# Broadcast rows of a selective scan: sixteen copies in DRAM instead of four, and one DMA instead of two for the group that mixes two directions

## The chip, the cores and the metric

The kernel runs on one core of a Trainium2 chip. The metric is the device time of the program in microseconds (us), the median of three runs. The profile is of one execution. Engines are named as in the profile: PE is TensorE, DVE is VectorE, ACT is ScalarE, POOL is GpSimd, and SP is SyncE, which here does nothing but issue DMAs; "SPq" is its queue of issues.

## The reference, cut to what matters

The program takes two images of 96 channels and 128 x 128 pixels. It normalizes over channels, adds the result of a four-direction selective state-space layer (a Mamba block for each direction, fused by one linear layer), and then runs two quantized feed-forward layers with a 3 x 3 convolution between them. The part that matters here is the scan of one direction over its L = 16384 positions, with 192 inner channels d and 16 states s:

```
xc  = silu(causal_conv4(x @ in_w.T))           # (L, 192)
dt  = softplus(xc @ Wdt + dt_b)                # (L, 192), through a rank of 6
B,C = xc @ xproj_w.T                           # (L, 16) each: the same for all channels d
h[d,s] = exp(dt[d] * A[d,s]) * h[d,s] + dt[d] * xc[d] * B[s]     # step after step
y[d]   = sum_s h[d,s] * C[s]
```

B and C depend on the position and the state, but not on the channel. With channels on partitions, a row B[s, :] has to stand on every partition.

## The kernel before

**Tiles.** For each image there are two passes (`pi`), each over a pair of directions: one along rows of the image, one along columns. Two times 192 channels make three groups of 128 partitions (`NG = 3`): group 0 is 128 channels of the first direction, group 2 is 128 channels of the second, and group 1, the middle one, has 64 channels of the first on partitions 0 to 63 and 64 of the second on 64 to 127. The positions are cut into 32 tiles of T = 512. So a pass has 32 steps, an image 64, the program 128.

**Steps and units.** A step is worked off in 24 units: three groups times eight pairs of states. One unit is, for 128 partitions and two states:

- POOL, `b_part` (L324): dt * xc * B, in place on the B rows, 128 x 1024;
- ACT, `decay` (L330): exp(dt * A), two instructions, into PSUM;
- DVE, `scan` (L334): two recurrences of 512 positions, one for each state;
- DVE (L409): h * C, 128 x 1024, in place on the C rows;
- ACT (L410): the last column of h, kept for the next step;
- PE, `sums` (L341): two matmuls by the identity, which add up over states in PSUM (`y`); a new `y` begins with L416, at the first unit of each group, and the old one is then multiplied by the gate on DVE (L349).

**Where the rows come from.** Once a step, the part of the prologue named `rows` computes all B and C rows of the next step: 64 of them (2 kinds, B or C; 2 directions; 16 states), on partitions 32 to 95 of the tile `rows`. `rows_out` copies them from PSUM and writes them to a DRAM tile, `bcd` (L261), four times over (`COPIES = 4`), with four DMAs of all 64 partitions. `row_tile` (L320) then fetches a quad, which is four states of B or of C and so enough for two units: 8 KB on each of 128 partitions, 1 MB. For groups 0 and 2 this is one DMA, whose source is read with a step of 0 so that the partitions take the four copies in turn. For group 1 it is two DMAs of 64 partitions, since the two halves read rows of different directions.

**Order.** Every engine's order is written out by hand (`manual_schedule`); SP issues DMAs in that order and waits at each for its buffer. The main loop runs over units k, and the fetches and the prologue of the next step are placed by unit:

```
if k % 2 == 0:
    fetch(k + 2 * B_AHEAD, 0, B_AHEAD, bs)      # B of units k+6, k+7; four buffers
feed(k + AHEAD)                                 # b_part of unit k+2
...                                             # scan, multiply of unit k-1, scan
if k % 2 == 0:
    fetch(k + 2 * C_AHEAD, 1, C_AHEAD, cs)      # C of units k+4, k+5; three buffers
```

`rows_out` of the next step stands at the end of unit 12 of a step. Unit 18 is the first that issues a fetch for the next step. Around the write SP's order is: B for unit 18, C for unit 16, the four writes of `bcd`, B for unit 20, C for unit 18, B for unit 22, C for unit 20, B for the next step's unit 0.

Of the kernel before, what the change touches and what calls it, by code (L numbers as in the profile page):

```python
# [10 lines left out]
F32 = mybir.dt.float32  # L11
# [12 lines left out]
T = 512  # L24
NT = L // T
R = T // W
S = 16
# [2 lines left out]
HID = 384  # L30
PAIRS = ((0, 2), (1, 3))
NG = 3
COPIES = 4
B_AHEAD = 3
C_AHEAD = 2
AHEAD = 2
# [1 line left out]
BCO = 32  # L38
NBC = 4 * S
# [3 lines left out]
def tile_metaformer(ctx: ExitStack, tc: tile.TileContext, a: dict, out: bass.AP):  # L43
    nc = tc.nc
# [138 lines left out]
    def mamba(acc, xnr, xnc):  # L183

        with ExitStack() as st:
# [3 lines left out]
            rows_d = pool("rows_d", 3, space=DRAM)  # L189
# [20 lines left out]
            def prologue(pi, i, d):  # L210
# [3 lines left out]
                src = []  # L214
# [40 lines left out]
                def rows_out():  # L255

                    d["rows"] = one.tile([BCO + NBC, T], F32, name="rows")
                    nc.scalar.copy(d["rows"], d["ps"][0 : BCO + NBC, :])
                    d["bcd"] = rows_d.tile([COPIES, 2, NBC // 2, T], F32, name="bcd")
                    for n in range(COPIES):  # L260
                        nc.sync.dma_start(d["bcd"][n].rearrange("k r t -> (k r) t"), d["rows"][BCO:, :])  # L261

# [35 lines left out]

                at = [(0, 0, load), (8, 1, partial(silu, "xc")), (14, 1, partial(silu, "sz"))]
                at += [(12, 0, rows), (12, 1, rows_out)]
                for g, k in enumerate((4, 5, 6)):
                    at += [(k, 0, partial(conv, g)), (k, 1, partial(conv_out, g))]
# [7 lines left out]
            def row_tile(d, g, s, k, ahead):  # L312

                t = gen.tile([128, 4, T], F32, name=f"row{k}", bufs=ahead + 1)
                for half in range(2) if g == 1 else (slice(None),):
                    rows = slice(half * 64, half * 64 + 64) if g == 1 else half
                    at = s + S * (half if g == 1 else g // 2)
                    n = (64 if g == 1 else 128) // COPIES
                    src = d["bcd"][None, :, k, at : at + 4, :].broadcast_to((n, COPIES, 4, T))
                    nc.sync.dma_start(t[rows], src)  # L320
                return t

            def b_part(d, g, b):
# [62 lines left out]
            def fetch(k, n, ahead, m):  # L386
                if k < total:
                    t = row_tile(state[k // nu], *units[k % nu], n, ahead)
                    m[k], m[k + 1] = t[:, 0:2, :], t[:, 2:4, :]
# [46 lines left out]
            for k in range(total + 6):  # L436
                n, u = divmod(k, nu)
# [185 lines left out]
```

## Time and profile before

| what | value |
|---|---|
| time, median of 3 runs | 13002.54 us (12999.16 to 13004.72) |
| profiled execution | 13002.5 us, TensorE clock 0.963 |
| busy | PE 83%, DVE 89%, ACT 66%, POOL 71% |
| scan, L334 | 5952 in 7339.4 us (mean 1274 ns), and a smaller form for the first step of a pass |
| multiply by C, L409 | 3072 in 3705.9 us (mean 1206 ns) |
| B part on POOL, L324 | 3072 in 7175.7 us (mean 2358 ns) |
| rows, 1 MB DMAs | 2048, 7.5 us from issue to landing (median) |
| rows, 512 KB DMAs | 2048, 8.0 us |
| `bcd` writes, 128 KB | 512, 9.8 us |
| DMA | 3400 MB in all, mean 262 GB/s, packets' time 83.1% of 16 engines' span |
| HBM | read 3288.94 MB, written 104.86 MB |

The page gives busy time for each engine, the costliest groups of instructions by line, and for each group how long its engine stood idle before it and what ended that. The wait tables sum such idle times by who waited for whom. "DMA share" in a window is the time that packets took on the core's 16 DMA engines, as a share of the window; a packet that takes longer because it shares a path counts longer. A landing time counts from the issue on SP and so includes the time behind earlier DMAs in the rings.

### The profile page before, as it was taken

What the parts mean: (1) busy time and instruction counts of PE and PEld (TensorE: products, weight loads), DVE (VectorE), ACT (ScalarE), POOL (GpSimd) and SP (SyncE); (2) the same over time, 40 slices, a digit from 0 to 9 for tenths busy, and PEclk for the clock granted to TensorE, in tenths of its full rate; (3) what the DMA queues carried; (4) which work ended last, traced back from release to release, by engine and by line L of the source; (5) the groups of instructions that cost most, each with busy time, mean ns of one, the idle gap of its engine ahead of it and who ended that gap; (6) DMA issues with size and microseconds to landing.
All of it is one profiled execution on the core that took longest, in us unless ns stands there. A gap on an engine that the chain in (4) does not pass through costs nothing. (4 is left out here: it accounts for less than half of the span.)

```text
span 13002.5 us, 97992 instructions
## 1 busy us (share of the span) xinstructions
PE 10850.3 (83%) x24208; PEld 3987.1 (31%) x24208; DVE 11569.1 (89%) x10865; ACT 8560.0 (66%) x14738; POOL 9215.4 (71%) x4772
## 2 busy tenths in 40 slices
PE   6888888888888888888978888888888888888889
PEld 2323233333333333333323333332333333333233
DVE  5999999999999999995459999999999999999954
ACT  6666666666666666665566666666666666666655
POOL 4877778777787787772147778777787777877721
PEclk8999999999999999999989999999999999999999
DMA  7999999999999999992079999999999999999920
GB/s 226 287 294 282 298 288 285 295 283 298 288 285 295 283 295 289 285 295 68 13 226 285 298 283 292 290 285 298 285 291 291 284 298 286 290 294 281 296 61 13
DMA packets 545331, 3400.40 MB, mean 262 GB/s; under 512 B 81612, under 2 KB 82732, under 8 KB 146840
## 3 DMA queue, kind: packets, MB, share of 16 engines
q1 hardware_dynamic: 544760, 3394.12, 83.1%
q8 instruction: 195, 3.19, 0.1%
q14 instruction: 376, 3.08, 0.1%
HBM read 3288.94 MB, written 104.86 MB: 261 GB/s over the span
## 5 line engine op out<-in xcount | busy, mean ns | idle before, releaser
L324 POOL TENSOR_TENSOR row<-dtu,row 128x1024 f32<-128x1024 f32 x3072 | 7175.7, 2358 | 1739.3 <-DMA row<-bcd 1419.2
L334 DVE TENSOR_TENSOR_SCAN da<-da,hst,row 128x512 f32<-128x512 f32 x5952 | 7339.4, 1274 | 351.2 <-ACT da L330 194.6
L341 PE MATMUL y<-row,ident 128*128 128x512 f32 x12288 | 6120.1, 626 | 1113.3 <-DVE row L409 1098.9
L330 ACT ACTIVATE da<-dt,amat 128x512 f32<-128x512 f32 x6144 | 4249.4, 692 | 207.5 <-ACT hst L410 0.4
L341 PEld LDWEIGHTS y<-row,ident 128*128 128x128 f32 x12288 | 2288.9, 197 | 4779.4 <-DVE row L409 2292.3
L409 DVE TENSOR_TENSOR row<-da,row 128x1024 f32<-128x1024 f32 x3072 | 3705.9, 1206 | 19.6 <-DMA row<-bcd 18.8
L410 ACT COPY hst<-da 128x2 f32<-128x2 f32 x3072 | 484.0, 158 | 2235.5 <-DVE row L409 2233.3
L416 PE MATMUL y<-xc,dmat 128*128 128x512 f32 x768 | 526.1, 773 | 779.1 <-DVE sz L349 779.1
L287 POOL TENSOR_TENSOR q<-e,q 128x512 f32<-128x512 f32 x384 | 488.0, 1271 | 821.8 <-ACT hst L410 709.1
L233 ACT ACTIVATE xc<-misc,convb 128x512 f32<-128x512 f32 x384 | 264.2, 688 | 1117.5 <-PE misc L207 1117.5
L207 PE MATMUL misc<-xa,inx 96*128 96x512 f32 (+1 forms) x2048 | 932.4, 597 | 59.0 <-DMA xa<-xnr 57.2
L207 PE MATMUL misc<-xb,inx 96*64 96x512 f32 (+1 forms) x2048 | 928.1, 595 | 1.6 <-ACT xc L233 1.6
L531 POOL TENSOR_TENSOR acc<-acc,y 96x512 f32<-96x512 f32 x128 | 147.6, 1153 | 987.0 <-DVE y L530 987.0
L541 PE MATMUL pc<-pad,kw 96*96 96x512 f32 x1152 | 566.7, 593 | 0.0
L207 PEld LDWEIGHTS misc<-xa,inx 96*128 96x128 f32 (+1 forms) x2048 | 323.6, 163 | 625.5 <-issue 493.4
L293 POOL TENSOR_TENSOR dt<-dt,ln 128x512 f32<-128x512 f32 x384 | 486.9, 1268 | 30.1
L297 POOL TENSOR_TENSOR dtu<-dt,xc 128x512 f32<-128x512 f32 x384 | 488.5, 1272 | 0.5
L290 POOL TENSOR_TENSOR ln<-ln,q 128x512 f32<-128x512 f32 x384 | 488.1, 1271 | 0.5
L359 PE MATMUL misc<-sz,gmat 128*96 128x512 f32 x1024 | 483.6, 594 | 0.0
L416 PEld LDWEIGHTS y<-xc,dmat 128*128 128x128 f32 x768 | 129.0, 211 | 1102.1 <-DVE sz L349 1099.1
L268 PE MATMUL misc<-rows,dtw 12*128 12x512 f32 x768 | 439.7, 652 | 18.5 <-ACT dt L275 17.2
L132 DVE TENSOR_TENSOR xq<-xm,rs 96x512 fp8e5<-96x512 f32 x128 | 87.9, 687 | 387.8 <-ACT rs L128 387.8
(75 smaller groups left out, 8403.8 us busy)
## 6 DMA issues: line engine op xcount, KB each, us to landing
row<-bcd SPq DMA_DIRECT2D x2048, 1024.0 KB, 7.5
row<-bcd SPq DMA_DIRECT2D x2048, 512.0 KB, 8.0
bcd<-rows SPq DMA_DIRECT2D x512, 128.0 KB, 9.8
xa<-xnr SPq DMA_DIRECT2D x124, 193.1 KB, 5.8
xb<-xnc SPq DMA_DIRECT2D x124, 193.1 KB, 5.5
acc<-in_x_dram SPq DMA_DIRECT2D x16, 768.0 KB, 17.8
xnr<-xn SPq DMA_DIRECT2D x16, 768.0 KB, 4.3
xnc<-stg SPq DMA_DIRECT2D x16, 768.0 KB, 5.6
```

Of the source, the lines that this page charges most:

```text
L207: nc.tensor.matmul(ps[rows, :], w(PAIRS[pi][d], k, lo, hi), src[d][:, k : k + T], **se)
L287: nc.gpsimd.tensor_tensor(d["q"], d["e"], d["q"], ALU.subtract)
L290: nc.gpsimd.tensor_tensor(d["ln"], d["ln"], d["q"], ALU.add)
L293: nc.gpsimd.tensor_tensor(d["dt"][g], d["dt"][g], d["ln"], ALU.add)
L297: nc.gpsimd.tensor_tensor(dtu, d["dt"][g], d["xc"][:, g, :], ALU.mult)
L324: nc.gpsimd.tensor_tensor(b, d["dtu"][g][:, None, :].broadcast_to((128, 2, T)), b, ALU.mult)
L330: nc.scalar.activation(da[:, j, :], d["dt"][g], AF.Exp, scale=amat[:, pi, g, s + j : s + j + 1])
L334: nc.vector.tensor_tensor_scan(h[:, j, :], da[:, j, :], b[:, j, :], 0.0 if i == 0 else hst[:, g, s + j : s + j + 1], ALU.mult, ALU.add,)
L341: nc.tensor.matmul(y, ident, c[:, j, :], start=False, stop=s + j == S - 1)
L409: nc.vector.tensor_tensor(c, h, c, ALU.mult)
L416: nc.tensor.matmul(y, dmat[:, pi, g, :], d["xc"][:, g, :], start=True, stop=False)
L541: nc.tensor.matmul(pc, kw[:, t, :], rows, start=t == 0, stop=t == 8)
```

## The change

`COPIES` becomes 16, and the DRAM tile is laid out anew: kind (B or C), then 32 copies, sixteen with the first direction's rows and after them sixteen with the second's, each copy with 16 states and one unused row. Group g reads sixteen copies from copy 8 * g on, one for every eight partitions. So group 0 takes the first direction alone, group 2 the second alone, and for group 1 partitions 0 to 63 fall on copies of the first direction and 64 to 127 on copies of the second: its quad is now one DMA over 128 partitions as well. The writing side is now one DMA for each kind and direction: it takes 16 partitions of `rows` and writes each sixteen times, 512 KB a DMA.

```diff
-COPIES = 4
+COPIES = 16
...
-                    d["bcd"] = rows_d.tile([COPIES, 2, NBC // 2, T], F32, name="bcd")
-                    for n in range(COPIES):
-                        nc.sync.dma_start(d["bcd"][n].rearrange("k r t -> (k r) t"), d["rows"][BCO:, :])
+                    d["bcd"] = rows_d.tile([2, 2 * COPIES, S + 1, T], F32, name="bcd")
+                    for n in range(4):
+                        to = d["bcd"][n // 2, n % 2 * COPIES : (n % 2 + 1) * COPIES, 0:S, :]
+                        r = d["rows"][BCO + n * S : BCO + (n + 1) * S, None, :].broadcast_to((S, COPIES, T))
+                        nc.sync.dma_start(to.rearrange("n s t -> s n t"), r)
...
-                for half in range(2) if g == 1 else (slice(None),):
-                    rows = slice(half * 64, half * 64 + 64) if g == 1 else half
-                    at = s + S * (half if g == 1 else g // 2)
-                    n = (64 if g == 1 else 128) // COPIES
-                    src = d["bcd"][None, :, k, at : at + 4, :].broadcast_to((n, COPIES, 4, T))
-                    nc.sync.dma_start(t[rows], src)
+
+                src = d["bcd"][k, COPIES // 2 * g : COPIES // 2 * g + COPIES, None, s : s + 4, :]
+                nc.sync.dma_start(t, src.broadcast_to((COPIES, 128 // COPIES, 4, T)))
                 return t
```

The number and order of all other instructions stay as they are.

## The prediction

> **What bounds the kernel now.** I read the page from the top: shares, slices, the costliest groups, then the table of waits, the DMA issues, and last one step of the scan in the timeline.
>
> ```profile
> PE 10850.3 (83%) x24208; PEld 3987.1 (31%) x24208; DVE 11569.1 (89%) x10865; ACT 8560.0 (66%) x14738; POOL 9215.4 (71%) x4772
> ...
> DVE  5999999999999999995459999999999999999954
> ...
> DMA  7999999999999999992079999999999999999920
> ```
>
> Two long stretches (the two images' scans) have both VectorE and the DMA engines at nine tenths. Which of them is the limit is told by who waits. Here is the wait table of the whole run, cut to VectorE in the scan and to GpSimd's wait for rows (columns: us in total, times, longest):
>
> ```profile
> POOL row L324 <- DMA row<-bcd: 1419.2, 331, 7.2
> ...
> DVE da L334 <- ACT da L330: 199.4, 126, 1.9
> DVE da L334 <- POOL row L324: 171.9, 8, 84.4
> DVE sz L349 <- PE y L341: 171.0, 128, 2.1
> DVE da L334 <- ACT hst L410: 139.4, 123, 1.6
> ...
> DVE row L409 <- DMA row<-bcd: 18.8, 28, 2.1
> ```
>
> GpSimd waits 1419 us for rows, but VectorE hardly notices: it waits 18.8 us for a C row, and of its 171.9 us for GpSimd two waits near 84 us (one at the start of each scan, before anything has been made) are nearly all. The other three come once a step, from ScalarE and TensorE, and no DMA is in them. In the stretch from 2000 to 5500 us VectorE is busy 3328.87 of 3500 us (95.1%) and runs 931 of the multiplies of line 409, so one unit (two scans and a multiply) takes 3.76 us and a step of 24 units 90.2 us. VectorE is the bound; rows arrive in time, some of them late for GpSimd but not for VectorE.
>
> Why GpSimd waits is in three windows of one step (columns: us of the window, busy time of each engine with its count, TensorE's clock, DMA share, GB/s):
>
> ```profile
> 3022.00:3032.00 10.00, 6.02 (x9) 2.53 (x10) 8.73 (x9) 6.26 (x13) 8.54 (x6) 0.72 1.03 426
> 3075.00:3081.00 6.00, 6.00 (x19) 2.43 (x16) 4.84 (x5) 2.12 (x4) 5.20 (x3) 1.00 1.01 228
> 3086.00:3095.00 9.00, 8.21 (x21) 2.70 (x19) 7.62 (x8) 8.05 (x11) 2.85 (x2) 1.00 1.04 232
> ```
>
> With full DMA engines, rows of the outer groups come at 426 GB/s (128 partitions in one DMA), those of the middle group at 228 to 232 (64 partitions in each). Half the partitions, half the rate.
>
> Last, one step around the writing of `bcd` (line 261), from the timelines of the DMA queue and of VectorE (start us, us, what):
>
> ```profile
> 3011.77 0.53 SPq L320 DMA_DIRECT2D row<-bcd  x1
> 3012.43 2.67 SPq L261 DMA_DIRECT2D bcd<-rows  x4
> 3015.69 0.57 SPq L320 DMA_DIRECT2D row<-bcd  x1
> 3017.53 0.56 SPq L320 DMA_DIRECT2D row<-bcd  x1
> ```
>
> ```profile
> 3030.19 1.21 DVE L409 TENSOR_TENSOR row<-da,row 128x1024 f32<-128x1024 f32 x1
> 3031.31 2.46 DVE L334 TENSOR_TENSOR_SCAN da<-da,hst,row 128x512 f32<-128x512 f32 x2
> 3033.67 1.21 DVE L409 TENSOR_TENSOR row<-da,row 128x1024 f32<-128x1024 f32 x1
> ```
>
> By the program's order these four issues are C for units 16 and 17, the next step's `bcd`, B for units 20 and 21, and C for units 18 and 19. A new `y` (line 416) starts in TensorE at 3027.96, so the multiply at 3030.19 is unit 17's and the one at 3033.67 unit 18's. The last of the four issues landed 11.1 us after issue, at 3028.6, and its first user came at 3033.67: 5.0 us to spare. Worked out from the same records for 122 inner steps, the mean is 5.05 us and the least 3.6.
>
> **What the Trainium skill says.** "SBUF — State Buffer", section "Door 1: The DMA port swizzle", says that a DMA's rate is set by how many of 16 SBUF ports its partitions reach: 64 partitions from 0 reach eight, 16 reach four, and it gives 104 GB/s for partitions 0 to 15 at 1 MiB (109 as the limit). The trace agrees where it can: half of 426 for 64 partitions. It shows no transfer of 16 partitions. For the reading side it shows the stores of the last stage (`out_dram<-acc`, 96 partitions) from 6000 to 6290 us: 4.0% of 16 engines' 290 us over 1632 packets of 2 KB (1904 less 272 small ones) is 114 ns a packet, where 2 KB at 426 GB/s / 1.03 / 16 takes 79 ns. So reads of SBUF collide too.
> "DMA: Bandwidth & Descriptors", section "Why a DMA increments its semaphore by 16 and not by 1", says that a DMA is split over as many engines (16 at most) as divide the slowest dimension of both sides. "Queues, rings and completion order" in the same page says that each engine takes its ring's descriptors in order. The trace agrees: at 3012 us the `bcd` writes wait 10 us behind rows issued before them.
>
> **The change part by part.**
> *One DMA for the middle group.* 2048 issues of 512 KB become 1024 of 1 MB over 128 partitions. In the step that is 8 MB at 414 GB/s (426 / 1.03) instead of about 225: 20 us of the queue's time instead of 37. VectorE gains what it waited on rows for: 18.8 us in the run, and nothing from GpSimd's 1419, which lie beside VectorE's work. The issues saved (0.53 us each on SyncE) are worth nothing, as SyncE mostly waits for buffers.
> *More copies for the readers.* An engine now reads its own copy. The outer groups already move at 426 GB/s with four copies, so I count nothing.
> *Sixteen copies to write.* A step wrote 4 x 128 KB from 64 partitions; it now writes 4 x 512 KB = 2.10 MB, each DMA from 16 partitions, with the partition as the slowest dimension of both sides. Each of 16 engines then reads one partition sixteen times, and those partitions (32 to 47, 48 to 63, 64 to 79, 80 to 95) lie on four ports at a time. Low end: no collision, 2.10 MB at 414 GB/s = 5.1 us. From this trace's two-to-a-port rate halved (115 GB/s): 18.2 us. From the page's 104 GB/s: 20.2 us. I take 20.2, as four engines on a port is the page's case.
> *What stands behind it.* The rows issued next lie in the same rings. With the middle group's backlog gone, the C of 3011.77 starts its packets some 1.2 us later (a small DMA lands in 2.1 us, part 6) and takes 2.53 us (1.05 MB at 414), to 3015.5. The four writes then hold all rings to 3035.7. B of unit 20 follows to 3038.2, C of unit 18 to 3040.8, landed at about 3041.1. Unit 18's multiply wants it at 3033.67 and waits 7.4 us; everything behind it on VectorE waits too. B of unit 20 comes late for GpSimd but within those 7.4 us. The next C (unit 20, issued before 3026) lands near 3046, and its user has moved past 3048: no second wait. The next step's first B now waits in SyncE for `bcd` to land (about 3036.5), and has over 10 us to spare.
> *The sum.* 126 steps have such writes during a scan (63 for each image): 126 x 7.4 = 932 us. At the start of each scan the writes take about 19 us more, mostly beside the chain that makes dt (GpSimd's first B part starts at 165.86 us, the `bcd` issue is at 140.52): about 3 us are left on VectorE's first C, 6 in all. 13002.5 + 932 + 6 - 19 = 13921.
>
> **The rivals.**
> *Hidden (12985 us).* The writes spread over all ports, or take under 12.8 us (20.2 less 7.4) for another reason; C of unit 18 is then in time and only the 18.8 us go: 0.14% less, no measurable change. For it: today's `bcd` writes are quick, and the split over engines of a 16-partition source is not in this trace. Against it: the 64-partition rows and the 114 ns of the stores both follow the ports.
> *Faster (12950 us).* The middle group's late B also delays something that the table puts down to ScalarE or TensorE, and some 50 us of those 510 us go. Against it: these waits come about 126 times, once a step, 1.1 to 1.6 us each, also where rows come early.
> *Far slower (19760 us).* The engines are split over the copies, so that all 16 read one partition at a time: 2.10 MB at 26 GB/s is 80 us, with rows (24 x 2.53) and inputs (2.5) 143 us a step, and the queue becomes the bound: 128 x 143, and the 1457 us outside (13002.5 less 128 x 90.2). Against it: the partition, not the copy, is the outer dimension.
>
> **How the numbers follow.** Port collision with its wait: 0.80. Hidden: 0.13. Faster: 0.04. Far slower: 0.03. The predicted time is the first's. In it, the writes' 18.2 to 21.5 us and the slack's spread give 5 to 9 us a step, 13620 to 14130; engines that run apart and share ports less would give 2 us, 13240. I draw the range from 13150 to 14250, which is nearly all of the first case and none of the others. Slower takes 0.80 + 0.03; the hidden case's gain of 0.14% could reach past 0.2%, so of 0.13 I give 0.02 to faster, with the 0.04.
>
> **What would show it.** Right: VectorE's wait for `row<-bcd` at the multiply grows from 18.8 to some 930 us in about 126 waits of 7 us; the `bcd` DMAs land after some 15 us in the median; HBM written goes from 104.86 to 306 MB (128 x 1.573 MB more); the middle group moves near 426 GB/s; VectorE in the scan falls from 95 to 88%. Wrong: a window over the `bcd` writes shows well over 115 GB/s, or VectorE has no wait there; then the ports do not bind for this split and the time stays near 12985.

## The result and the profile after

The changed kernel takes 15281 us (15243 to 15310 in four runs) against 13002 us: a ratio of 1.175, with a 95% interval of 1.172 to 1.178. The direction was forecast, the size was not: 2279 us more instead of 919, outside the range. Runs more than 1.5% above the fastest of their kernel count as slow and are left out; below that is one run, of e7.

From the page of the changed kernel, the shares, two rows of slices, the DMA queue and HBM:

```profile
PE 11714.6 (77%) x24208; PEld 4197.7 (28%) x24208; DVE 11671.8 (77%) x10865; ACT 8621.3 (57%) x14738; POOL 9225.4 (60%) x4772
...
DVE  4777788887788877876458878777888778787764
...
DMA  8999999999999999994089999999999999999940
...
q1 hardware_dynamic: 626680, 3595.38, 92.9%
...
HBM read 3288.94 MB, written 306.18 MB: 236 GB/s over the span
```

VectorE has fallen from nine tenths to seven or eight in the scan; the DMA engines have not fallen. HBM written is the 306 MB that was forecast. But the packets' share of the queue rose from 83.1 to 92.9%, where the forecast's quicker rows and longer run would have lowered it. The first lines of the wait table, cut to those of interest:

```profile
POOL row L323 <- DMA row<-bcd: 3949.5, 1147, 10.6
...
DVE row L408 <- DMA row<-bcd: 2625.1, 1252, 12.4
```

VectorE's wait for C rows went from 18.8 us in 28 waits to 2625.1 us in 1252. The forecast was some 930 us in about 126 waits, one a step: there are ten a step. So the writes of `bcd` cannot be the whole cause; rows come late all through the step. Taken apart by unit, 824 us (128 waits) lie before the multiply of unit 18, where the forecast put its wait; the rest is spread over the other even units. The DMA issues say the same (KB each, median us to landing):

```profile
row<-bcd SPq DMA_DIRECT2D x3072, 1024.0 KB, 18.8
bcd<-rows SPq DMA_DIRECT2D x512, 512.0 KB, 17.5
```

A row DMA landed after 7.5 us before and takes 18.8 now. Windows of the changed kernel: the first writes of `bcd`, the first rows (all of group 0, with no other packets beside them), the long stretch, rows alone in one step, and a stretch in which a later write and rows are mixed:

```profile
141.50:144.00 2.50, 1.58 (x2) 0.01 (x1) 0.00 (x0) 2.49 (x2) 0.00 (x0) 0.50 0.94 99
156.00:170.00 14.00, 0.00 (x0) 0.00 (x0) 3.58 (x3) 6.07 (x10) 13.54 (x9) 0.50 1.01 228
2000.00:5500.00 3500.00, 2694.17 (x5480) 959.54 (x5478) 2856.90 (x2475) 2022.76 (x3465) 2331.31 (x1191) 0.91 1.01 261
3020.00:3035.00 15.00, 15.00 (x43) 5.70 (x41) 11.58 (x10) 7.28 (x13) 5.12 (x4) 1.00 1.02 244
3066.00:3069.00 3.00, 1.49 (x5) 0.57 (x4) 3.00 (x3) 2.87 (x6) 1.16 (x1) 1.00 0.99 378
```

The first `bcd` writes move at 99 GB/s: the four ports of the prediction (it took 104). But the rows of group 0, a 128-partition DMA that ran at 426 GB/s before, now move at 228 GB/s with nothing beside them, and in the long stretch the DMA share is 1.01: the DMA engines are the bound. And in the last window 378 GB/s are moved. By the trace's packet records (all packet times here and below are from them), rows take about a third of the DMA engines' time in it and the write two thirds; the 2 KB packets of the write average 84 ns there, against 309 in the first window. Over the run they average 95. So the reads lost half their rate, and after the first write the writes hardly collided.

Where the 2252 us between the two profiled runs lie: the wait for C rows is 2606 us longer; the three once-a-step waits of VectorE (for `da` and the state's copy from ScalarE, for `y` from TensorE) went from 510 to 61 us, as the other engines catch up while VectorE waits for rows; and VectorE's busy time, counted without overlaps, grew by 103. 2606 less 449 plus 103 is 2260.

### The profile page after: what moved, and what is told of

Its sections match the earlier page's. It is cut to its first block, busy times and chain, and to the rows that moved or that the text cites. A ratio compares the mean times of both kernels' runs of the same rounds, so it can differ in the third digit from the quotient of the medians.

```text
span 15254.5 us, 95686 instructions
## 1 busy us (share of the span) xinstructions
PE 11714.6 (77%) x24208; PEld 4197.7 (28%) x24208; DVE 11671.8 (77%) x10865; ACT 8621.3 (57%) x14738; POOL 9225.4 (60%) x4772
## 3 DMA queue, kind: packets, MB, share of 16 engines
q1 hardware_dynamic: 626680, 3595.38, 92.9%
## 5 line engine op out<-in xcount | busy, mean ns | idle before, releaser
L340 PE MATMUL y<-row,ident 128*128 128x512 f32 x12288 | 6885.0, 693 | 2163.2 <-DVE row L408 2132.7
L408 DVE TENSOR_TENSOR row<-da,row 128x1024 f32<-128x1024 f32 x3072 | 3733.9, 1215 | 2644.2 <-DMA row<-bcd 2625.1
L340 PEld LDWEIGHTS y<-row,ident 128*128 128x128 f32 x12288 | 2487.6, 216 | 6386.3 <-DVE row L408 3759.1
L207 PE MATMUL misc<-xa,inx 96*128 96x512 f32 (+1 forms) x2048 | 969.1, 617 | 190.3 <-DMA xa<-xnr 160.4
L356 PE MATMUL misc<-acc,ident 96*96 96x512 f32 x512 | 377.0, 821 | 35.4 <-ACT dt L277 35.4
## 6 DMA issues: line engine op xcount, KB each, us to landing
row<-bcd SPq DMA_DIRECT2D x3072, 1024.0 KB, 18.8
```

Source lines behind the costliest of these rows:

```text
L207: nc.tensor.matmul(ps[rows, :], w(PAIRS[pi][d], k, lo, hi), src[d][:, k : k + T], **se)
L340: nc.tensor.matmul(y, ident, c[:, j, :], start=False, stop=s + j == S - 1)
L408: nc.vector.tensor_tensor(c, h, c, ALU.mult)
```

## The experiments

Two theories for the reads. *Ports*: what matters is how many the source counts on the outside; the old row DMA counts 32 x 4 (32 times four copies), the new one 16 x 8 (sixteen copies, eight partitions each), and with 16 the partitions are dealt out over the DMA engines so that two engines meet on a port of SBUF (one of the 16 ways into it, of which the prediction speaks) all the time. *Place*: the copies' addresses in DRAM, or one engine reading one copy eight times, are slow to read.

**Only the outer count, in the kernel before (e1).** Eight copies written (1 MB a step instead of 0.5), and groups 0 and 2 read 16 x 8: the source runs through the same eight copies sixteen times.

```diff
-COPIES = 4
+COPIES = 8
...
-                    n = (64 if g == 1 else 128) // COPIES
-                    src = d["bcd"][None, :, k, at : at + 4, :].broadcast_to((n, COPIES, 4, T))
+                    m = 4 if g == 1 else COPIES
+                    src = d["bcd"][None, 0:m, k, at : at + 4, :].broadcast_to((16, m, 4, T))
```

> The kernel before with eight copies, each read by all engines; for groups 0 and 2 the source now counts 16 x 8 instead of 32 x 4, the middle group is fetched as before. Ports (the source's outer count decides how partitions are dealt out over engines; with 16 an engine gets eight neighbours and two engines meet on a port): a 1 MB row DMA of the outer groups needs about 4.6 us instead of 2.5, all groups move near 230 GB/s with full engines, time 15000 to 15700 us. Place (the sixteen copies' addresses in DRAM, or one engine reading one copy eight times, are slow to read): rows of the outer groups stay near 426 GB/s, time within 0.5% of before.

16727 us, a ratio of 1.286 (1.284 to 1.288), beyond even what *ports* expected. The long stretch of this kernel in one window:

```profile
2000.00:5500.00 3500.00, 2575.67 (x4859) 909.24 (x4860) 2540.62 (x2198) 1806.20 (x3081) 2067.49 (x1054) 0.86 1.01 223
```

All groups move at the rate that the halves of the middle group had. *Place* falls for this kernel: the copies are as far apart as before, and none is named eight times in a row.

**Only the outer count, in the changed kernel (e2).** `COPIES = 32`: 32 copies for each direction, each read by four partitions, so the source counts 32 x 4. The writes double to 4 MB a step.

```diff
-COPIES = 16
+COPIES = 32
```

> The changed kernel with COPIES = 32, so the source counts 32 x 4, the writes are 4 MB a step. Ports: rows of all groups move near 426 GB/s; the writes take 10 us or more a step, time between 13000 and 13700 us. Place: rows stay as slow as in the changed kernel (same pitch of copies, one engine still reads few copies many times) and the writes add 5 us or more a step: 15900 us or more.

15976 us, 1.229 (1.227 to 1.230): the time is that of *place*, and yet the trace says *ports*. Two windows, rows alone and the writes, and VectorE's first wait:

```profile
3045.00:3059.00 14.00, 12.93 (x31) 4.46 (x30) 12.67 (x12) 11.67 (x18) 6.83 (x4) 1.00 0.94 358
3070.00:3090.00 20.00, 14.76 (x26) 5.24 (x26) 13.75 (x13) 12.25 (x20) 9.60 (x6) 0.83 0.95 119
```

```profile
DVE row L408 <- DMA row<-bcd: 2912.5, 128, 25.8
```

Rows move fast again, at 358 GB/s with a share of 0.94 (8 KB packets take 309 ns in the median, against 314 in the kernel before and 544 in the changed kernel). What costs the time is the writes: 128 waits, one a step, of 22.8 us in the mean, all but two of them before the multiply of unit 18. Here they do collide, at 119 GB/s: 4.19 MB take 35.2 us, and less the 12.8 us that the prediction found free, that is 22.4. So this run also tests the prediction's own mechanism, and it holds.

**The writes alone (e3).** Sixteen copies are written as in the change; rows are read in the old pattern, from four of them, in two DMAs for the middle group.

```diff
-                src = d["bcd"][k, COPIES // 2 * g : COPIES // 2 * g + COPIES, None, s : s + 4, :]
-                nc.sync.dma_start(t, src.broadcast_to((COPIES, 128 // COPIES, 4, T)))
+                for half in range(2) if g == 1 else (slice(None),):
+                    rows = slice(half * 64, half * 64 + 64) if g == 1 else half
+                    at = COPIES * (half if g == 1 else g // 2)
+                    n = (64 if g == 1 else 128) // 4
+                    src = d["bcd"][None, k, at : at + 4, s : s + 4, :].broadcast_to((n, 4, 4, T))
+                    nc.sync.dma_start(t[rows], src)
```

> The writing side of the change alone: sixteen copies are written as in the change, rows are read in the old pattern (32 x 4 from four of the copies, two DMAs for the middle group). Both theories: rows of the outer groups near 426 GB/s. If the writes go in lockstep, four engines to a port (307 ns for 2 KB, as the changed kernel's first burst began), they take 13 us or more and the time is 13500 to 14000 us; if the engines fall apart and the writes take some 6 us, 13000 to 13300 us.

14029 us, 1.078 (1.077 to 1.080), just above the higher of the two expected ranges. VectorE's wait:

```profile
DVE row L412 <- DMA row<-bcd: 1040.4, 169, 10.4
```

Taken apart by unit over 122 inner steps, 7.96 us of it a step lie before the multiply of unit 18, where the prediction put 7.4. That the sizes agree is partly chance: the 2 KB packets of the writes average 168 ns, so that the 64 of an engine take 10.8 us, not 20. The middle group's backlog, which this kernel still has and the prediction had taken away, makes up the difference: in the mean the C row ahead of the writes landed 62.5 us after the step's start here, and 57.8 in a kernel without the backlog (e5, below).

**The distance of the copies (e4).** The changed kernel without the unused row, copies 32 KB apart instead of 34.

```diff
-                    d["bcd"] = rows_d.tile([2, 2 * COPIES, S + 1, T], F32, name="bcd")
+                    d["bcd"] = rows_d.tile([2, 2 * COPIES, S, T], F32, name="bcd")
```

> The changed kernel without the unused seventeenth row: copies 32 KB apart instead of 34 KB. Ports: within 1% of the changed kernel. Place: if the distance of copies matters, the time moves by over 2% one way or the other.

15383 us (15378 to 15428), 1.183 (1.181 to 1.185): 0.7% above the changed kernel: within the 1% of *ports*, and less than the 2% that would have been a sign of *place*. The unused row may be worth something, but it is not the cause.

**All reads 32 x 4 (e5).** The middle group in one DMA as in the change, but from all 32 copies, four partitions each; the outer groups from four copies with an outer step of 0. Writes as in the change. This kernel is what the prediction thought the change to be.

```diff
-                src = d["bcd"][k, COPIES // 2 * g : COPIES // 2 * g + COPIES, None, s : s + 4, :]
-                nc.sync.dma_start(t, src.broadcast_to((COPIES, 128 // COPIES, 4, T)))
+                if g == 1:
+                    src = d["bcd"][k, :, None, s : s + 4, :]
+                else:
+                    at = COPIES * (g // 2)
+                    src = d["bcd"][None, k, at : at + 4, s : s + 4, :]
+                nc.sync.dma_start(t, src.broadcast_to((32, 4, 4, T)))
```

> The changed kernel with its reads dealt as 32 x 4 for every group: groups 0 and 2 read four of the sixteen copies with an outer step of 0, the middle group reads all 32 copies, four partitions each, still in one DMA. Writes as in the change. Ports: all rows near 426 GB/s, no 64-partition transfer is left. If the four engines on a port stay in step as the prediction held, the writes take 20 us a step and the time is 13900 us; if they fall apart as in e3 (168 ns a packet in the mean, 11 us), C of unit 18 is in time or nearly so and the time is 12990 to 13150 us. Place: rows of the middle group (34 KB apart) stay slow, over 13500 us.

13429 us, 1.033 (1.031 to 1.034): between the two cases of *ports*, and under what *place* asked. Two windows, rows of an outer group and the middle of a write, and VectorE's wait:

```profile
3004.00:3008.00 4.00, 3.22 (x8) 1.25 (x7) 2.67 (x4) 3.95 (x4) 0.00 (x0) 1.00 1.01 426
3026.00:3034.00 8.00, 3.97 (x8) 1.35 (x8) 6.73 (x7) 7.78 (x12) 2.29 (x2) 1.00 0.97 176
```

```profile
DVE row L412 <- DMA row<-bcd: 421.3, 126, 4.9
```

126 waits, one for each write, 3.3 us each. All of it lies before the multiply of unit 18. Place and number are the prediction's; the size is not. In the mean of 122 inner steps the C row ahead of the writes landed 57.8 us after the step's start and the last write 71.1: the writes hold the queue for some 13.4 us, not 20.2, as they move at neither 104 GB/s (always four to a port) nor 414.

**All reads 32 x 4 and the writes spread (e6).** As e5; and the rows are ordered by state in their tile, so that each write takes every fourth partition from 32 to 95 instead of sixteen neighbours.

```diff
-                        r = d["rows"][BCO + n * S : BCO + (n + 1) * S, None, :].broadcast_to((S, COPIES, T))
+                        r = d["rows"][BCO + n : BCO + NBC : 4, None, :].broadcast_to((S, COPIES, T))
...
-                to = slice(BCO + (2 * j + k) * S, BCO + (2 * j + k + 1) * S)
+                to = slice(BCO + 2 * j + k, BCO + NBC, 4)
```

> As e5, and the rows are ordered by state in their tile, so that each write takes every fourth partition from 32 to 95 instead of sixteen neighbours. If the ports of the sources set the time of the writes, they take 5.4 us a step (84 ns for 2 KB), no wait is left at unit 18, and the time is 12985 us within 15, 0.1% less than before. If something else slows the writes, the same time as e5.

12999 us in 13 runs, 0.9997 (0.9989 to 1.0005): no difference from the kernel before. The 2 KB packets average 86 ns (164 in e5), and VectorE has no wait for C rows among its waits; the `bcd` writes land after 8.8 us in the median (12.0 in e5). The stretch of both, this kernel first, then the kernel before:

```profile
2000.00:5500.00 3500.00, 2925.16 (x6426) 1070.15 (x6425) 3328.58 (x2912) 2360.90 (x4079) 2733.17 (x1399) 0.97 0.83 308
```

```profile
2000.00:5500.00 3500.00, 2930.39 (x6428) 1070.63 (x6427) 3328.87 (x2911) 2363.18 (x4083) 2736.91 (x1400) 0.97 0.92 290
```

The DMA share has fallen from 0.92 to 0.83, though more bytes move, and VectorE is busy 3328.58 us instead of 3328.87. What the change was for is reached here in part (GpSimd still waits 899 us for rows, 1419 before), and it is worth nothing, because VectorE had no wait to give. This was the one version that could have beaten both; it equals the kernel before.

**The changed kernel with its writes spread (e7).** Writes as in e6, reads 16 x 8 as in the change.

> The changed kernel with the same spreading of its writes, reads as in the change (16 x 8). Ports: the rows collide as before and set the pace alone: 15000 to 15350 us. If it was the writes that made the changed kernel slow, under 13500 us.

15051 to 15208 us in three runs, a ratio of 1.164 (1.159 to 1.169), against 1.175 (1.172 to 1.178) of the changed kernel. Spreading the writes (87 ns a packet) gives back about 1%; the reads set the pace.

**More outer counts (e8, e9).** The kernel before with `COPIES = 2` (outer groups 64 x 2) and with `COPIES = 1` (a plain step of 0 over 128).

> The kernel before with COPIES = 2, so that groups 0 and 2 are read as 64 x 2, the halves of the middle group as 32 x 2. If it is a source of 16 alone that is dealt badly, rows of the outer groups stay near 426 GB/s and the middle group near 230, time within 0.5% of before. If only 32 is dealt well, rows of the outer groups take about 4.6 us, over 15000 us. If fewer copies are slower to read, something between.

> The kernel before with COPIES = 1: one copy, the source a plain outer step of 0 over 128 partitions (64 for the halves of the middle group). If a source of 16 alone is dealt badly, rows of the outer groups stay near 426 GB/s, time within 1% of before. If fewer copies are slower to read, as e8 (13085 us, one run) may hint, more than 13085 us.

13085 and 13065 us, one run each: 0.6 and 0.5% more than before, e8 just beyond what was expected. 8 KB packets have medians of 315 and 318 ns, as with 32 x 4 (314). So over 128 partitions 32, 64 and 128 on the outside are fast, and 16 is not. The halves of the middle group now count 32 and 64 on the outside and seem to have stayed slow: over a third of the row packets still take more than 400 ns, 619 and 608 in their mean (590 in the kernel before). VectorE's wait for C rows is 149.5 and 135.2 us in these two, against 18.8, while its wait for the state's copy is 63 and 54 us shorter; that is about the difference. Why fewer copies are a little slower is open.

**Which partitions, with a source of 16 (e10).** The kernel before, a quad of an outer group in three DMAs: partitions 32 to 95 (16 x 4), 0 to 31 and 96 to 127 (16 x 2 each).

```diff
-                for half in range(2) if g == 1 else (slice(None),):
-                    rows = slice(half * 64, half * 64 + 64) if g == 1 else half
-                    at = s + S * (half if g == 1 else g // 2)
-                    n = (64 if g == 1 else 128) // COPIES
-                    src = d["bcd"][None, :, k, at : at + 4, :].broadcast_to((n, COPIES, 4, T))
-                    nc.sync.dma_start(t[rows], src)
+                parts = ((0, 64, 0), (64, 64, 1)) if g == 1 else ((32, 64, g // 2), (0, 32, g // 2), (96, 32, g // 2))
+                for lo, size, dd in parts:
+                    at = s + S * dd
+                    m = size // 16
+                    src = d["bcd"][None, 0:m, k, at : at + 4, :].broadcast_to((16, m, 4, T))
+                    nc.sync.dma_start(t[lo : lo + size], src)
```

> The kernel before, but a quad of an outer group comes in three DMAs, each with a source of 16: partitions 32 to 95 (16 x 4), 0 to 31 (16 x 2) and 96 to 127 (16 x 2); the middle group as before. Ports: the first of the three reaches every port once and runs at 309 ns for 8 KB, the other two meet two to a port, 610 ns; with the middle group's 610 the mean is about 510 ns, a step's rows take 98 us and the time is 14000 to 15000 us. If it is the number of partitions that counts, no packet of rows is under 610 ns in the mean and the time is 16500 us or more.

15403 us (1.184; 1.181 to 1.187), in neither range; packets average 550 ns. The time doesn't decide, but the first transfers of the run do, when the DMA engines start together: windows over the first DMA of partitions 32 to 95, over the 32-partition DMAs that follow it, and over the second of the first kind:

```profile
144.60:146.20 1.60, 0.00 (x0) 0.00 (x0) 0.00 (x0) 1.59 (x2) 0.00 (x0) 0.50 0.87 338
146.70:148.40 1.70, 0.00 (x0) 0.00 (x0) 0.00 (x0) 0.99 (x2) 0.59 (x1) 0.50 0.97 227
148.50:149.50 1.00, 0.00 (x0) 0.00 (x0) 0.00 (x0) 0.40 (x1) 0.92 (x2) 0.50 0.97 401
```

Divided by their DMA shares these are 389, 234 and 413 GB/s: 64 partitions from 32 on are fast, 32 partitions are not, with the same outer count. Later in the run few row packets are fast (559 ns in the median); that DMA engines then work on different DMAs at once and slow each other is a reading that was not tested.

## Why the prediction was wrong

*What bounds the kernel before* was right: in e6 VectorE has no wait for C rows left, GpSimd waits 899 us for rows instead of 1419, and the time is the same. One sign was read too strongly, without weight in the sum: the stores' 114 ns a packet, taken to show that reads of SBUF collide, is a mean; their median is 86 ns, about that of the spread writes (e6).

*One DMA for the middle group* failed: it was to move near 426 GB/s. The rows of the changed kernel move at 228 to 261, about as the halves did, since their source is 16 x 8.

*More copies for the readers* is the step that made the error: "The outer groups already move at 426 GB/s with four copies, so I count nothing." The same edit turned their source from 32 x 4 into 16 x 8. A step has 24 row DMAs of 128 packets; at the 309 ns of e5's median they take 59.3 us over 16 engines, at the measured mean of 524 ns they take 100.6. With the writes' 6.1 us (64 packets an engine at 95 ns) and the inputs' 1.9 (12 packets at 159) this is 109 us a step in the queue, against the 90.2 that VectorE needs. The step became 108 us long ((15254.5 - 1457) / 128). I had applied the port rule to the writes only, and took a DMA over all 128 partitions to be out of its reach.

*Sixteen copies to write*: the mechanism was right, with its place, its number of waits and its victim, and three terms were mis-sized. With all reads fast (e5) a step waits 3.3 us and not 7.4. The burst takes 13.4 us instead of 20.2, which alone would leave 0.6; but the C row ahead of it landed 5.7 us after its issue (3.7 in the forecast), and the two rows behind it took 6.1 us (5.4 in the forecast). In all it costs some 426 us there (13429 less 13002) where 932 were forecast; alone (e3) it costs 1027, with the row ahead later still. In the changed kernel it hides: there the writes' packets average 95 ns, and e7 shows that their collisions are worth about 1%. That the DMA engines come to the write out of step, and so to different ports, is my reading of the first write (309 ns a packet) against the later ones; the trace doesn't tell engine from engine.

*The rivals.* "Hidden" is what e6 measures, 12999 against 12985, but for another kernel. None had the reads slowed by their own form, so none was near.

Shown: 16 on the outside of a 128-partition source halves the rate (e1 against before, e2 and e5 against the changed kernel), wherever the copies lie. The rate of sixteen source partitions depends on which they are (e5 against e6), and that of a source of 16 on the partitions it fills (e10). Over 128 partitions 16 on the outside is also eight on the inside; no run tells the two apart. Argued only: the deal itself. If with 16 each engine takes eight neighbouring partitions, then by the port table of the Trainium skill ("SBUF — State Buffer", "Door 1: The DMA port swizzle"), which e10 (389 to 413 GB/s against 234) and e6 (86 ns a packet against 164) agree with, the engines come in pairs that share the same two ports: partitions 0 to 7 and 32 to 39, for one. Which partitions an engine took stands in no trace here. Open too is why the row packets of e1 take 598 ns in the mean and those of the changed kernel 524.

## What to carry to other kernels

The form of a DMA's source can decide its rate as much as its partitions do: over 128 partitions a broadcast written with 16 on the outside ran at about half the rate of the same bytes with 32, 64 or 128. A DMA that reads few partitions of SBUF should take them far apart: sixteen that were every fourth of 64 took half the time a packet of sixteen neighbours (86 ns against 164). And before speeding up a late transfer, look for who stands still: GpSimd's 1419 us of waiting were worth nothing, as VectorE waited 19.

## What the runs showed of the hardware that was not expected

A collision had no fixed price. Packets of the same four writes took 309 ns at first, with no other packets beside them; 164 ns in the mean behind rows that are fast (e5); and 95 behind rows that are slow (the changed kernel), where a window shows rows and the write side by side. That DMA engines out of step stop colliding fits this, and is not shown. The cost worked out for engines in step (20.2 us) was half as much again as what e5 measured (13.4).

And issuing took longer behind these writes. The first writes and the rows behind them in the changed kernel, in the timeline of SyncE's queue:

```profile
138.50 8.45 SPq L263 DMA_DIRECT2D bcd<-rows  x4
147.12 9.30 SPq L319 DMA_DIRECT2D row<-bcd  x6
```

Four issues took 8.45 us where they took 2.67 in the step shown of before. In e5 the last of the four writes and the two row DMAs after it took 3.5 to 4.0 us each to issue in the mean, instead of some 0.5 in the kernel before; C for unit 18 was issued 4.9 us later in the step than before (62.9 against 58.0 us). As the writes still held the queue then, this cost nothing.
